# Four-layer gated model on one core: layer 2's mixture by kept picks in blocks of 256, in place of all experts on all tokens

## The chip, the cores and the metric

The kernel runs on one core of a Trainium2 chip, as one program. The metric is the device time of an execution in microseconds. The engines are named as the profile names them: PE is the matrix engine (PEld its weight loads), DVE the vector engine, ACT the scalar engine, POOL the general engine that also issues indirect DMAs, SP the engine that here issues all other DMAs.

## The reference

Four layers follow one another on an activation x of 4 batches x 512 tokens x 256 features, all float32. Each layer adds a gated attention over a context and then a gated feed-forward part, both on a layer norm of x:

```python
x = x + tanh(g_xattn[l]) * attention_l(layernorm(x), ctx)
x = x + tanh(g_ffn[l]) * ffn_l(layernorm(x))
```

Attention 0 is a recurrence over 512 steps (an attention and two LSTM cells in each step); attention 1 is a two-way gated attention; attention 2 is additive (a tanh of the sum of a projected token and a projected context row); attention 3 has 16 heads. The feed-forward part 0 is a mixture with the best expert of 8, part 1 with the best two, part 3 a matrix product on values quantised to 8 bits. The one that is changed is part 2. It keeps, for each token, the experts of highest probability as long as their cumulative probability is under 0.8, and always the best:

```python
probs = softmax(x @ Wr + br)
mask = cumsum(sorted(probs)) < 0.8;  mask[..., 0] = True
gate = probs * keep                                   # keep: mask in the order of the experts
h = relu(einsum('bth,ehf->betf', x, W1) + b1)         # 256 -> 1024, 8 experts
y = einsum('betf,efh->beth', h, W2) + b2              # 1024 -> 256
out = einsum('bte,beth->bth', gate, y)
```

An expert that a token doesn't keep has gate 0 and so adds nothing to it.

## The kernel before, in words

P = 128 is the number of partitions, S = 512 the tokens of a batch, D = 256 the features (KD = 2 pieces of 128), TPB = 4 the pieces of 128 tokens in a batch. The tokens x stay in the chip's memory as `xtok`, 16 pieces of 128 x 256.

**The first part** (`lstm`, `recurrence`) runs the 512 steps of layer 0's attention. What has no place in a step's chain, layer 0's own mixture above all, is put as small tasks into a planner (`Later`) that fills the gaps of the engines. Its weights come through `fetch` and `take`, from SP. This part ends some 3600 us after the start.

**The rest** ("the tail", layers 1 to 3) is written as Python generators, each of which yields after a few instructions. `weave(main, side, ratio)` takes a step of the main generator and then `ratio` steps of the side one, until both have ended; `run` takes one alone; `chain` puts several one after the other. PE's instructions keep the order in which they are written (`InOrder`, L913); the other engines' order is decided by the scheduler of the framework. PSUM is shared by pools of 3 banks for `ps_up`, 2 for `ps_down`, 2 for everything else (`ps_side`) and 1 accumulator. All matmuls of the tail are recorded at L921, so that they are told apart by tile.

- `norm` (L952) makes the layer norm `xn` of a batch and its transpose `xT`.
- `ranked` (L1001) makes the router's values and each expert's rank; `ready_moe` (L1037) adds the keep rule, `comb` (gate times tanh of the layer's factor) and the b2 term.
- `moe` (L1074) is layer 2's mixture for one batch: for each of 8 experts, 8 pieces of 128 hidden features, each two matmuls of 512 columns and a relu on ACT (L1085); then for each of the 4 token pieces, 8 matmuls of 256 columns, whose sum DVE multiplies by the expert's column of `comb` and adds to `xtok` (L1092). All tokens go through all experts. An expert's up and down weights are 1 MB each and are loaded once per batch by SP into two pools of three buffers.
- `Picks`, `picks`, `picked` and `back` (L1113 to L1342) are layer 1's mixture, which works on chosen tokens alone. The tokens are in two groups of 1024. `picks` counts each expert's tokens with two matmuls, makes a place for each (token, expert) pick on DVE, and turns places into a list of tokens by 16 matmuls of one-hot matrices made on DVE (`hot` L1221, `val` L1223). `picked` runs 20 blocks of 128 picks, each gathering its rows by an indirect DMA (`xg`, L1261) from a copy of the normed rows in DRAM, and writes the products to `res` in DRAM (L1311); a branch behind it (L1320) would run up to three more blocks. `back` gathers two rows per token (`yg`, L1331) and adds them to `xtok` with their weights (L1336).
- `additive` (L1544) is layer 2's attention of a batch: 128 ACT tanh (L1565) of 128 x 512, each reduced by PE into `psr`.
- `context_l3`, `heads` (L1693) and `quantised` (L1756) are layer 3: keys and values of the context, then per batch the 16 heads, then the quantised product and the output.

The order of the tail is written out in `gated_blocks_kernel` (L1793): 

1. layer 1's attention and picks of group 0, alone;
2. layer 1's blocks of group 0, woven 1:1 with attention and picks of group 1 and layer 2's context;
3. layer 1's blocks of group 1, woven 1:2 with the gathering back of group 0, `additive` of batch 0, `ready_moe` of batch 0, `additive` of batch 1;
4. `moe` of batches 0, 1, 2 and 3, each woven with what is ready: batch 0 with the gathering back of group 1, `additive` 2 and `ready_moe` 1; batch 1 with `additive` 3 and `ready_moe` 2; batch 2 with `ready_moe` 3, layer 3's context and layer 3 of batches 0 and 1; batch 3 with layer 3 of batch 2;
5. layer 3 of batch 3, alone.

## Time and profile before

| what | value |
|---|---|
| median of three runs | 5609.78 us (5602.8 to 5616.77) |
| the profiled execution | 5608.65 us |
| its span, from the first to the last instruction | 5606.9 us |
| granted PE clock, mean over the span | 0.976 of full speed |
| PE busy | 4908.2 us, 88% of the span |
| DVE, ACT, POOL busy | 2364.6, 2586.2, 284.2 us |
| 0 to 3600 us (recurrence): PE busy | 3077.5 us |
| DMA | 312.55 MB, mean 56 GB/s |
| packets of the indirect DMAs (queue q0) | 3456, 9.44 MB |

A row of the page's groups names a line of the kernel, an engine, an operation, what it writes and reads, how often, its busy time and the mean duration of one. A row of the table by stage gives, for a stretch of the span, the busy time of each engine, the granted PE clock, the share of the DMA engines' time and what they moved. Ends of matmuls are modelled, so that busy times of groups of matmuls overlap a little. Idle time of an engine is put down to the event that ended it.

### The profile page before, as it was taken

The page shows a single profiled execution, that of the slowest core. Times are in us where ns is not written, and L with a number is a line of the kernel's source. Part 1 is how long each engine was busy: PE and PEld are TensorE (multiplying, and loading weights), DVE is VectorE, ACT ScalarE, POOL GpSimd, SP SyncE. Part 2 cuts the span into 40 slices and gives each one's busy share as a digit, 9 for nine tenths or more (in the row PEclk, how much of TensorE's full clock was granted, in tenths as well). Part 3 has the DMA queues.
Part 4 walks back from the last instruction along what each step waited for, and adds up shares of the span by engine and source line. Part 5 has one row for each costly group of instructions (what it writes and reads, how often), then busy time and mean ns, then how long its engine had stood idle before and what let it go on. Part 6 is the DMA issues. An engine that isn't in the chain of part 4 may idle for free. (4 is left out here: it accounts for less than half of the span.)

```text
span 5606.9 us, 137186 instructions
## 1 busy us (share of the span) xinstructions
PE 4908.2 (88%) x57896; PEld 2594.7 (46%) x57896; DVE 2364.6 (42%) x9440; ACT 2586.2 (46%) x7090; POOL 284.2 (5%) x700
## 2 busy tenths in 40 slices
PE   5556798889998899999999899879899999999997
PEld 2222344344444444444444346745344565655664
DVE  4555555555555555555555553144332011232223
ACT  2323464465655665665665565212466545212221
POOL 1000000100000100000000100000101000000000
PEclk9999999999999999999999999979899999999997
DMA  3000010101111111111111112225443112110100
GB/s 114 2 2 2 10 55 32 36 32 39 47 52 39 39 51 40 43 54 40 48 42 40 44 46 97 80 69 177 148 143 115 61 63 92 53 49 31 63 33 5
DMA packets 72766, 312.55 MB, mean 56 GB/s; under 512 B 11361, under 2 KB 27122, under 8 KB 46386
## 3 DMA queue, kind: packets, MB, share of 16 engines
q1 hardware_dynamic: 68690, 294.31, 15.2%
q8 instruction: 454, 7.44, 0.6%
q0 software_dynamic: 3456, 9.44, 0.5%
q14 instruction: 166, 1.36, 0.1%
HBM read 292.18 MB, written 10.22 MB: 54 GB/s over the span
## 5 line engine op out<-in xcount | busy, mean ns | idle before, releaser
L852 PE MATMUL psf<-fw,alb 128*4 128x256 f32 x8192 | 538.4, 380 | 156.4 <-DVE alb L848 125.9
L705 PE MATMUL ps_up<-xm,up 128*128 128x256 f32 x2048 | 614.8, 412 | 3.4 <-ACT h L715 3.3
L736 PE MATMUL ps_down<-down,h 128*128 128x256 f32 x2048 | 580.6, 399 | 0.0
L810 PE MATMUL psf<-whh,hb 128*4 128x256 f32 x8176 | 538.3, 381 | 0.0
L921 PE MATMUL ps_up<-xT,up 128*128 128x512 f32 x1024 | 480.7, 610 | 0.0
L921 PE MATMUL ps_down<-down,h 128*128 128x256 f32 x2048 | 462.0, 382 | 0.0
L705 PEld LDWEIGHTS ps_up<-xm,up 128*128 128x128 f32 x2048 | 335.9, 188 | 226.7 <-issue 174.1
L840 ACT ACTIVATE al<-psr,stat 128x64 f32<-128x64 f32 x1024 | 312.4, 309 | 269.9 <-DVE stat L839 269.3
L736 PEld LDWEIGHTS ps_down<-down,h 128*128 128x128 f32 x2048 | 356.9, 189 | 156.9 <-issue 111.6
L819 ACT ACTIVATE e<-e 128x256 f32<-128x256 f32 x512 | 213.4, 417 | 465.4 <-DVE e L818 464.3
L921 PEld LDWEIGHTS ps_down<-down,h 128*128 128x128 f32 x2048 | 385.0, 190 | 85.4 <-issue 22.2
L801 PE MATMUL psa<-wh,hb 128*4 128x64 f32 x8176 | 208.6, 220 | 228.5 <-DVE hb L878 227.2
L839 DVE TENSOR_REDUCE stat<-psr 128x1 f32<-128x64 f32 x1024 | 229.4, 224 | 417.4 <-PE psr L828 406.6
L818 DVE TENSOR_TENSOR e<-fproj,hw 128x256 f32<-128x256 f32 x1024 | 395.1, 427 | 17.6
L828 PE MATMUL psr<-e,vrep 128*32 128x64 f32 x16384 | 348.7, 223 | 49.0 <-ACT e L819 43.5
L1565 ACT ACTIVATE h<-featT,txtT 128x512 f32<-128x512 f32 x512 | 328.5, 711 | 134.7 <-PE psr L921 125.7
L459 PE MATMUL psf<-ge,ident 128*4 128x256 f32 x4096 | 318.0, 382 | 65.4 <-DVE gt L860 65.2
L828 PEld LDWEIGHTS psr<-e,vrep 128*32 128x32 f32 x16384 | 261.1, 109 | 238.1 <-ACT e L819 230.7
L863 ACT ACTIVATE ga<-gt 128x32 f32<-128x32 f32 x512 | 116.8, 228 | 524.9 <-DVE gt L860 524.7
L860 DVE STREAM_TRANSPOSE gt<-psf 128x256 f32<-128x256 f32 x512 | 230.1, 449 | 301.1 <-PE psf L852 300.5
L852 PEld LDWEIGHTS psf<-fw,alb 128*4 128x4 f32 x8192 | 116.6, 84 | 502.4 <-DVE alb L848 502.1
L1085 ACT ACTIVATE h<-ps_up,m_b 128x512 f32<-128x512 f32 x256 | 175.4, 686 | 375.6 <-PE ps_up L921 375.4
(391 smaller groups left out, 6014.3 us busy)
## 6 DMA issues: line engine op xcount, KB each, us to landing
up<-in_L_w_dram SPq DMA_DIRECT2D x96, 1024.0 KB, 4.9
down<-in_L_w_dram SPq DMA_DIRECT2D x96, 1024.0 KB, 4.9
up<-in_L_w_dram SPq DMA_DIRECT2D x80, 512.0 KB, 4.6
down<-in_L_w_dram SPq DMA_DIRECT2D x40, 512.0 KB, 3.7
res<-y SPq DMA_DIRECT2D x40, 128.0 KB, 6.1
xtok<-in_x_dram SPq DMA_DIRECT2D x4, 512.0 KB, 4.0
xh<-in_x_dram SPq DMA_DIRECT2D x32, 64.0 KB, 2.3
xtok<-xh SPq DMA_DIRECT2D x32, 64.0 KB, 2.0
```

The source lines that it names most:

```text
L459: net.tc.keep_in_program_order(net.nc.tensor.matmul(out[32 * q : 32 * q + NB, :], lhsT=sel, rhs=ge[t // 32][:, ts(q, 256)], start=True, st ...
L705: yield nc.tensor.matmul(cell["ps"][:, f % 2, :], lhsT=ex["w"][:, k, ts(f, P)], rhs=box["x"][:, k, :], start=k == 0, stop=k == KD - 1,)
L736: yield nc.tensor.matmul(cell["ps"], lhsT=ex["h"][:, f, ts(p, P)], rhs=ex["down"][:, f, :], start=f == 0, stop=f == 7,)
L810: pin(nc.tensor.matmul(psf[32 * q : 32 * q + NB, :], lhsT=h[:, c, :], rhs=w["whh"][:, c, ts(q, 256)], start=False, stop=False,))
L818: pin(nc.vector.tensor_add(e[:, p], w["fproj"][:, p], bc(hw[:, :, ts(p, 2)], 3, SC)))
L828: pin(nc.tensor.matmul(ps["r"][p][ts(2 * b + i, 32), :], lhsT=w["vrep"][:, c, :], rhs=ev[:, ::-1, :] if i else ev, start=c == 0, stop=c == ...
L839: pin(nc.vector.tensor_reduce(stat[:, p, 0:1], ps["r"][p], AX.X, ALU.max, negate=True))
L840: pin(nc.scalar.activation(al[:, p], ps["r"][p], AF.Exp, bias=stat[:, p, 0:1], accum_out=stat[:, p, 1:2]))
L852: pin(nc.tensor.matmul(psf[32 * q : 32 * q + NB, :], lhsT=alb[:, p], rhs=w["fw"][:, p, ts(q, 256)], start=False, stop=p == 1,))
L860: pin(nc.vector.transpose(gt.rearrange("p g b -> p (g b)"), psf))
L921: return lambda *a, **k: self.tc.keep_in_program_order(fn(*a, **k))
L1565: nc.scalar.activation(h, featT[:, ec, :], AF.Tanh, bias=w["txtT"][:, ec, col : col + 1])
```

## The change

Layer 2's mixture is computed for kept picks alone, in the manner of layer 1's, and both layers share the code.

- **Groups and kinds.** Layer 2 too works on two groups of 1024 tokens. A `Kind` holds for a layer how many picks a token has at most (2 and 6), the size of a block (128 and 256 picks), how many blocks always run (20 and 20), and how many each nested branch adds (3 and 4), up to 23 and 31 blocks in all.
- **Places.** `picks` makes counts by two matmuls, as before, and a place for each of a token's `most` picks on DVE. The one-hot matmuls and the token list are gone.
- **Putting rows in place.** The normed rows themselves (`xs`) are written to the picks' places in a DRAM array `rows` by indirect DMAs from POOL (L1225 of the new kernel): for each of 8 pieces of 128 tokens, `most` DMAs of 128 rows of 1 KB. That is 16 in a group of layer 1 and 48 in one of layer 2. They are declared independent of each other. A pick that isn't kept goes to a row of its own behind the blocks. A block's rows are then read by one plain DMA on SP (L1277), and each such load waits for all puts of its group.
- **Blocks.** `Blocks` loads rows and weights by the block's expert (a value read by SP), into one ring of three buffers for up and down weights, which replaces the weight pools of the whole kernel. A layer-2 block is 4 transposes, 16 matmuls of 256 columns, 16 relus shared between ACT and DVE, 16 matmuls of 256 columns, and two copies of 128 x 256 (one on DVE, one on ACT) that SP writes to `res`.
- **Branches.** After the sure blocks, `rest` reads the number of blocks and opens nested branches, with one buffer each.
- **Back.** `back` gathers six rows for each piece of 128 tokens in layer 2, 48 per group, through four buffers.
- **Scratch.** All of `rows` and the part of `res` that the sure blocks don't write are filled from x by DRAM-to-DRAM DMAs on SP when the recurrence starts. These are 2 x (14080 + 2817 + 2944 + 385) rows of 1 KB, 41 MB.
- **Order of the tail.** Layer 1's blocks of group 1 are woven 1:2.7 with group 0's gathering back, attention 2 and picks; layer 2's blocks of group 0 1:1.5 with the same of group 1; its blocks of group 1 1:0.75 with the gathering back of group 0, layer 3's context and the first 95 steps of layer 3 of batches 0 and 1. Then `turns` alternates the rest of that, followed by layer 3 of batch 3, with layer 3 of batch 2, which gets the ring's memory and `ps_up`'s banks (`over=True`).

The diff, cut to its core:

```diff
-        self.weights = ctx.enter_context(tc.tile_pool(name="weights", bufs=3))
+        self.ring = keep.tile([P, 3, 2, 2048], FP, name="ring")
+        self.at = {"up": 0, "down": 0}
         self.ready = {part: deque() for part in ("up", "down")}
         self.coming = {part: deque() for part in ("up", "down")}
-        self.expect(0, NBLK)
...
+    def scratch(self, name, rows, unset):
+        x = self.dram.tile([rows, D], FP, name=name)
+        while unset < rows:
+            n = min(NT, rows - unset)
+            self.nc.sync.dma_start(x[unset : unset + n, :], self.a["x"][0:n, :])
+            unset += n
+        return x
...
+KINDS = {1: Kind(1, 2, 128, 20, 3), 2: Kind(2, 6, 256, 20, 4)}
...
+class Kind:
+    def __init__(self, layer, most, size, sure, step):
+        self.layer, self.most, self.size, self.sure, self.step = layer, most, size, sure, step
+        self.all = GB * S * most // size + NE - 1
+        self.none = self.all * size
+        self.rows = self.none + (most * GB * S if most > 2 else 0)
...
     ps = t.ps(P, 2, GJ, NE)
-    mm(nc, ps[:, 0], [(pk.upper, sel)])
-    mm(nc, ps[:, 1], [(pk.ones, sel)])
...
+    place, index = tile("place", kind.most, GJ), tile("index", kind.most, GJ, dt=I32, of="got")
+    cw = tile("cw", kind.most, GJ, of="got")
+    at = tile("at", GJ, NE)
+    for k in range(kind.most):
+        v.scalar_tensor_tensor(at, rank, float(k), pos, ALU.is_equal, ALU.mult)
+        v.tensor_reduce(place[:, k, :], at, AX.X, ALU.add)
+    v.tensor_copy(index, place)
+    to = index
+    if layer == 2:
+        away, to = tile("away", kind.most, GJ), tile("to", kind.most, GJ, dt=I32)
+        v.scalar_tensor_tensor(away, place, kind.none - 0.5, pk.each, ALU.is_gt, ALU.mult)
+        v.tensor_add(away, away, place)
+        v.tensor_copy(to, away)
+    out["put"] = []
+    for j in range(GJ):
+        for k in range(kind.most):
+            x = nc.gpsimd.indirect_dma_start(
+                out=rows[:, :], out_offset=bass.IndirectOffsetOnAxis(ap=to[:, k, j : j + 1], axis=0),
+                in_=xs[:, j, :], in_offset=None,
+            )
+            for y in out["put"]:
+                net.tc.declare_no_dep(x.ins, y.ins, reason="each pick has a place of its own")
+            out["put"].append(x)
+    yield
...
-    ps = t.ps(P, NP1)
-    for k in range(2):
-        for j in range(GJ):
-            hot = two.tile([P, P], FP, name="hot")
-            v.tensor_scalar(hot, pk.col, place[:, k, j : j + 1], None, ALU.is_equal)
-            val = two.tile([P, NP1], FP, name="val")
-            v.tensor_scalar(
-                val, pk.col[:, 0:NP1], blk[:, k, j : j + 1], pk.tok[:, j : j + 1],
-                ALU.is_equal, ALU.mult,
+    v.tensor_copy(tile("expert", kind.all, dt=I32, of="got"), eb)
+    v.tensor_reduce(tile("sum", 1), nb, AX.X, ALU.add)
+    v.tensor_copy(tile("blocks", 1, dt=I32, of="got"), out["sum"])
+    for k in range(kind.most):
+        v.scalar_tensor_tensor(at, rank, float(k), comb, ALU.is_equal, ALU.mult)
+        v.tensor_reduce(cw[:, k, :], at, AX.X, ALU.add)
...
+        b["x"] = self.t.rows[:, at]
+        x = sp.dma_start(
+            b["x"][:, 0 : kind.size // P, :],
+            got["rows"][ts(i, kind.size), :].rearrange("(h p) d -> p h d", p=P),
+        )
+        for y in got["put"]:
+            net.tc.add_manual_dep(
+                x.ins, y.ins.name,
+                mybir.DependencyInfo(mybir.DependencyClass.Sync, mybir.DependencyReason.DATA),
+                reason="the rows' places are known on the chip alone",
             )
...
+    def work_2(self, lo, hi, at):
+        t, nc, w, pool = self.t, self.t.nc, self.w, self.pool
+        nf = F_MOE[2] // P
+        for i in range(lo, hi):
+            b = w[i]
+            h = pool.tile([P, nf, 256], FP, name="h_2")
+            for fp in range(nf // 2):
+                ps = t.up.tile([P, 2, 256], FP, name="ps_up", tag="up")
+                for n in range(2):
+                    f = 2 * fp + n
+                    mm(nc, ps[:, n, :], ((b["up"][:, k, ts(f, P)], b["xT"][:, k, :]) for k in range(KD)))
+                    if n:
+                        nc.vector.tensor_scalar(
+                            h[:, f, :], ps[:, n, :], b["b1"][:, f : f + 1], 0.0, ALU.add, ALU.max
+                        )
+                    else:
+                        nc.scalar.activation(h[:, f, :], ps[:, n, :], AF.Relu, bias=b["b1"][:, f : f + 1])
+                yield
+            self.behind(i, hi, "up", at)
+            if i + 1 < hi:
+                self.turn(w[i + 1])
+                yield
+            for half in range(2):
+                ps = t.down.tile([P, D], FP, name="ps_down", tag="down")
+                mm(nc, ps, ((h[:, f, ts(half, P)], b["down"][:, f, :]) for f in range(nf)))
+                self.out(i, half, ps)
+                if half:
+                    self.behind(i, hi, "down", at)
+                yield
...
+    def rest(self):
+        kind, net = self.kind, self.t.net
+        n = net.nc.values_load(self.got["blocks"][0:1, 0:1], min_val=0, max_val=kind.all)
+        at = (self.first + kind.sure + 2) % 3
+        def go(lo):
+            if lo < kind.all:
+                with net.tc.If(n > lo):
+                    hi = min(lo + kind.step, kind.all)
+                    run(self.some(lo, hi, at))
+                    go(hi)
+        go(kind.sure)
...
+    for b in batches:
+        for i in range(TPB):
+            j = (b - group[0]) * TPB + i
+            for k in range(kind.most):
+                y = pool.tile([P, D], FP, name="yg", bufs=4)
+                nc.gpsimd.indirect_dma_start(
+                    out=y[:, :], out_offset=None, in_=got["res"][:, :],
+                    in_offset=bass.IndirectOffsetOnAxis(ap=got["index"][:, k, j : j + 1], axis=0),
+                )
+                xj = net.xtok[:, b * TPB + i, :]
+                nc.vector.scalar_tensor_tensor(
+                    xj, y, got["cw"][:, k, j : j + 1], xj, ALU.mult, ALU.add
+                )
+            yield
...
-            run(layer1(0))
-            weave(picked(t, pk, pairs[0]), chain(layer1(1), context_l2(t, w2, p2)), 1.0)
...
+            run(picks_of(1, 0, l1))
+            weave(b0.sure(), chain(picks_of(1, 1, l1), context_l2(t, w2, p2)), 1.1)
+            b0.rest()
...
-        weave(
-            picked(t, pk, pairs[1]),
-            chain(back(t, pk, 0, pairs[0]), additive(t, w2, p2, 0), second(0), additive(t, w2, p2, 1)), 2.0,
-        )
-        net.expect(2, NB)
-        for _ in range(3):
-            net.fetch()
-        weave(moe(t, m2, 0, got[0]), chain(back(t, pk, 1, pairs[1]), additive(t, w2, p2, 2), second(1)), 1.0)
-        weave(moe(t, m2, 1, got[1]), chain(additive(t, w2, p2, 3), second(2)), 1.0)
...
+        weave(b1.sure(), chain(back_of(1, 0), picks_of(2, 0, l2)), 2.7)
+        b1.rest()
+        weave(c0.sure(), chain(back_of(1, 1), picks_of(2, 1, l2)), 1.5)
+        c0.rest()
...
-        return chain(heads(t, w3, p3, b), quantised(t, w3, p3, b, out))
-    weave(
-        moe(t, m2, 2, got[2]),
-        chain(second(3), context_l3(t, w3, p3), layer3(0), layer3(1)), 1.35,
-    )
-    weave(moe(t, m2, 3, got[3]), layer3(2), 0.6)
-    run(layer3(3))
+    def layer3(b, over=False):
+        return chain(heads(t, w3, p3, b, over), quantised(t, w3, p3, b, out))
+    start = chain(back_of(2, 0), context_l3(t, w3, p3), layer3(0), layer3(1))
+    weave(c1.sure(), part_of(start, 95), 0.75)
+    c1.rest()
+    run(turns(
+        chain(start, back_of(2, 1, [3]), layer3(3)),
+        chain(back_of(2, 1, [2]), layer3(2, True)),
+    ))
```

## The prediction

> **What bounds the kernel now.** I read the slices of the page first, then its groups, then a table by stage, then the chain of waits and the POOL timeline in single stages. In the slices, each 140 us long, TensorE is only half to nine tenths busy in the first 26 (the recurrence, which the diff leaves alone but for its start) and full in the ones that hold layer 2.
>
> ```profile
> PE   5556798889998899999999899879899999999997
> PEclk9999999999999999999999999979899999999997
> ```
>
> The table by stage (columns: stretch, its length, then busy us and count of PE, PEld, DVE, ACT, POOL, granted clock, DMA share, GB/s) covers everything after the recurrence and the first layer-1 attentions:
>
> ```profile
> 3741.00:3966.00 225.00, 206.42 (x756) 121.44 (x756) 98.79 (x262) 46.14 (x77) 17.85 (x19) 0.96 0.44 147
> 3966.00:4010.00 44.00, 21.66 (x40) 9.68 (x40) 16.19 (x39) 5.23 (x7) 21.00 (x22) 0.61 0.58 200
> 4247.00:4274.00 27.00, 16.90 (x37) 7.62 (x37) 15.51 (x48) 7.55 (x15) 11.91 (x13) 0.81 0.67 260
> 4274.00:5491.00 1217.00, 1187.43 (x4725) 728.36 (x4724) 247.61 (x572) 413.48 (x643) 1.09 (x1) 0.99 0.16 56
> 5491.00:5607.00 116.00, 77.21 (x321) 52.02 (x320) 42.61 (x81) 21.16 (x33) 0.00 (x0) 0.69 0.01 5
> ```
>
> The 1217 us of layer 2's mixture are PE time: 1187 busy at a clock of 0.99. So a matmul removed there comes off the end one for one. The stretches that lose time are the seams: the first weave's end (44 us with 22 busy, clock 0.61), the second's (27 with 17), and layer 3's last batch alone (116 with 77, clock 0.69). The chain (start, us, what) gives the price of a piece with nothing modelled in it; I use it and not the busy sums of the groups, whose modelled ends overlap (480.7 + 462.0 = 942.7 us):
>
> ```profile
> 5434.99 10.50 PE ps_up L921 x24
> 5445.49 3.45 PE ps_down L921 x16
> ```
>
> **Removed: 32 (expert, batch) pieces.** 24 records of ps_up are 12 matmuls of 512 columns in 10.50 us, so four take 3.50; 16 records of ps_down are 8 matmuls of 256 columns in 3.45. A piece has 16 of the first and 32 of the second: 4 x 3.50 + 4 x 3.45 = 27.8 us, x32 = 890.
>
> **Added: 40 blocks of 256.** A block has 16 up matmuls and 16 down matmuls, all of 256 columns: 32 x 3.45/8 = 13.8 us, and four transposes of rows (x8 records took about 1.05 us at full clock): 14.85, x40 = 594. The reference's inputs give 4333 kept picks in the first 1024 tokens, by expert 35, 996, 965, 641, 66, 991, 155, 484: 1+4+4+3+1+4+1+2 = 20 blocks; the second group also fills 20. The nested branches are never entered, and a token keeps at most 5, so the sixth pick is always spare work. **Saved: 890 - 594 = 296 us.**
>
> Here a rule speaks against the change. The Trainium skill, "TensorE: Matmul & The Clock Gate", section "Why this matters for your kernels", asks that narrow matmuls (M under 512) be padded or looped densely over K, or the clock oscillates. The change halves the width of ps_up. At half clock all the time the 594 would be 1188, and the kernel about 300 us slower than before. The row for it is ps_down: 256 wide, 3.45 us for 16 records in the middle of a stretch whose clock is 0.99. I take the row; width alone costs nothing while PE has a queue.
>
> **Added: indirect DMAs on POOL, and the seams.** Today's 72 (40 xg, 32 yg) become 128 scatters (2 x 16 and 2 x 48) and 128 gathers. The POOL timeline (start, us, engine, line, operation, idle before it) at the second seam:
>
> ```profile
> 4245.29 0.96 POOL L1331 DMA_INDIRECT yg<-res,g_index  x1 [0.30 <-issue]
> 4246.55 0.95 POOL L1331 DMA_INDIRECT yg<-res,g_index  x1 [0.30 <-issue]
> ```
>
> One each 1.26 us where nothing is waited for; 16 gathers with four buffers and their additions took 25.4 us, 1.6 each. No scatter is in the trace. The nearest row is this gather: 1.26 from issue to issue, and a median of 4.3 from issue to landing (2.7 to 6.1). From below a scatter can't be cheaper than POOL's 0.95. From above, each is paid to its landing. The skill, "DMA: Bandwidth & Descriptors", "Anatomy of one DMA - SWDGE (gpsimd) path", has 2.0 us fixed plus bytes/436e3, 2.3 us for 128 KB, mostly the receipt of the write and most for HBM, the target here. One after another, 48 would take 110 us by it, 60.5 by the row. The scatters are declared independent, so I take the row, and the rule for the upper side. Seam by seam, with PE kept in program order and the place of each instruction read off the changed kernel's order:
>
> - First: token lists took 3727 to 3738 (16 one-hot pairs), the gather 3.2 more. Now 16 scatters, 20 us, about 4 to land and 2.5 for the row load: +12.5. The second group's lists disappear from the first weave, where they held PE some 12 us: net 0.
> - First weave to second: the branch and the wait for weights stay as in the 44 us stretch. 0.
> - Layer-1 blocks to layer-2 blocks: the scatters follow their counts by about 11 us on DVE; 60.5 + 4 + 2.5 to the first row load: first transposes at +79. PE has two layer-1 blocks left (about 22 us): 56 idle, which replaces the 10 idle of 4247 to 4274. +46.
> - First to second half of layer 2: same queue, with 40 us of blocks left. 45 idle, less what the old kernel lost here, nothing. Layer 3's 4 MB of weights stand ahead of block 1's on SP: at about 400 GB/s some 8 us more. A memset of context_l3 stands on DVE behind all scatters and ahead of the last relu, so the last down matmuls (7 us) fall behind the wait; that is inside the 45. +53.
> - End: layer 3 of batch 2 needs 24 gathers of 1.6 us, the last landing (4) and a norm (6), while about 8 us of batch 1 are left: 40 idle, and 28 later, where batch 3 runs out its own chain. The old end idled 39. +29.
> - Clock: after the idle of 3966 to 3973, eight records took 6.68 us instead of 3.50. Three new idles: 3 x 4 = +12.
> - The second half's additive attentions now stand beside 20 blocks where they stood beside 16 pieces of twice the PE work. A batch has 128 tanh of 0.71 us, two batches 182 us of ACT, plus relus and copies, under 380 of PE. I charge +15 for places where the weave meets ACT, and +6 for the gathers that the second group's norm waits for, behind POOL's scatters.
>
> Sum: -296 + 0 + 46 + 53 + 29 + 12 + 21 = -135.
>
> At no cost: the fills. 41 MB from DRAM to DRAM go out on SP at the recurrence's start; the DMA view shows 2 GB/s from 70 to 560 us and SP's next issue at 665, so they need some 65 GB/s; the first slice moved 227 GB/s at a share of 0.63. At half that pace they end some 600 us late, the first mixture's weights queue behind them on SP, and the work that fills the recurrence's gaps runs after it instead: up to 600 us. Sixteen relus of half the old width (0.69 us for 512) are some 6 us on two engines under 13.8 of PE, two copies of y replace two additions into xtok (0.49); uncovered they would cost about 1 us a block, 40 in all. DVE's loops for places (12 operations of about 0.25) are counted in the 11 us. Block traffic is 2.25 MB per 14.85 us, 151 GB/s, against 400 seen.
>
> **How the numbers follow.** The profiled execution took 5608.65 us with a span of 5606.9, so 1.7 lie outside the span; the median, 5609.8, is 1.1 above it. 5606.9 - 135 + 1.7 + 1.1 = 5475.
>
> - Forecast, seams as priced: 5475. Chance 0.60, own range 5430 to 5520.
> - The seams hide better: if the picks finish early enough in each weave that POOL's 60 us run under blocks, 46 + 45 and most of the clock's 12 go: about 5380. The order speaks against it (the picks end two blocks before the weave does), the unknown pace of PE in the weave for it. 0.12.
> - Scatters at the rule's 2.3 us: 1.04 more for each of the 96 of layer 2, which are exposed, is +100, and 17 more if the first seam's 16 are too: 5575 to 5590. Speaks for it: HBM writes with receipts; against: the four independent gathers at 1.26. 0.15.
> - Slower than before: POOL waits for each scatter before the next (the ring, or a dependency that the declaration does not lift). At the landing of 4.3 us, (4.3 - 1.26) x 112 exposed = +340: about 5815. The turn is at 135/112 = 1.2 us above the row, 2.5 us per scatter. Against it: the gathers' 0.30 gaps and two landings in flight. 0.08, with the fills delaying the recurrence inside it.
> - It doesn't do what it says: 21 blocks in a group would run a branch with one buffer, each block waiting for 2 MB (about 25 us in series), up to 100 us a group, 5575 to 5675. The count excludes it unless rounding moves picks over a boundary (the first group's expert 5 has 991 of 1024, expert 6 155 of 256: far off). 0.02. A time within 0.3% of before, which is about what a measurement of this kernel can tell from no change: 0.03 of all.
>
> The range leaves out the lower half of the well-hidden case, the slow case and what lies beyond: 5390 to 5590. Faster by over 0.3%: 0.88; within: 0.03; slower: 0.09.
>
> **What the profile after would show.** PE's groups: layer 2's up and down matmuls of 256 columns, 1280 records each of ps_up and ps_down in the 40 blocks, about 3.45 us for 16 at a clock of 0.99; two idle PE stretches of 45 to 60 us, ended by a row load; POOL with 48 DMA_INDIRECT in a row at 1.26; an idle of about 40 us before batch 2's norm. I am wrong if the gaps on POOL exceed 0.3 us, if blocks stand more than 16 us apart with PE idle inside (weights or x rows late), or if the recurrence ends later than it does now.

## The result, and the profile after

The changed kernel takes 5827.24 us, the median of four runs (5819.72 to 5830.31), against 5607.39 for the kernel before on the same chip: a ratio of 1.0388 [1.037, 1.0406]. It is slower. The profiled execution took 5819.72 with a span of 5818.0, at a mean clock of 0.941. The forecast span was 5606.9 - 135 = 5471.9, so the miss is 346 us.

The slices of the changed kernel, 145 us each:

```profile
PE   3455689889999899999999899868884888398857
PEclk7899999999999999999999999889996999699967
```

Where layer 2 stood at 9s before, slices 31 and 35 (the seams) are at 4 and 3 tenths, the three slices between at 8, and the clock is 6 in both seams and in slice 39, near the end. The table by stage, for the row of scatters ahead of layer 2's first group, its blocks, the seam between the groups, the second group's blocks, and the end (columns as before):

```profile
4407.00:4475.00 68.00, 0.00 (x0) 0.00 (x0) 5.24 (x13) 0.00 (x0) 49.36 (x52) 0.53 0.54 187
4475.00:4938.00 463.00, 400.96 (x1928) 259.68 (x1928) 112.13 (x310) 219.95 (x382) 20.56 (x22) 0.97 0.32 108
4938.00:5032.00 94.00, 17.26 (x66) 13.10 (x66) 8.45 (x21) 2.54 (x6) 39.48 (x41) 0.60 0.45 168
5032.00:5524.00 492.00, 424.05 (x1860) 313.99 (x1860) 138.36 (x290) 80.66 (x155) 40.71 (x41) 0.97 0.32 104
5524.00:5818.00 294.00, 191.42 (x840) 126.15 (x840) 131.89 (x278) 54.38 (x85) 47.16 (x48) 0.72 0.11 28
```

The two seams hold 145 us without PE (68 and 94 - 17), where the forecast had 109. In the two block stages PE is idle for 62 and 68 us although the clock is 0.97.

The first seam is the row of 48 scatters and what follows it: POOL's last scatter, SP's loads of the blocks' rows, and PE's first transposes.

```profile
4458.34 0.96 POOL L1225 DMA_INDIRECT rows<-g_xs,g_to  x1 [0.31 <-issue]
4472.07 3.49 SPq L1277 DMA_DIRECT2D rows_in<-rows  x3
4475.09 1.09 PE L932 MATMUL ps_side<-ident,rows_in 128*128 128x128 f32 x4 [68.10 <-DMA rows_in<-rows]
```

The load went out 12.8 us after the last scatter was issued (4458.34 + 0.96), where 4 had been forecast. The PE timeline about the second seam (start, us, what, idle before it and what ended it) shows two more kinds of loss:

```profile
4911.65 7.07 PE L932 MATMUL ps_down<-ring,h 128*128 128x256 f32 x32
4918.56 1.03 PE L932 MATMUL ps_up<-xT,ring 128*128 128x256 f32 x4
4920.20 1.99 PE L932 MATMUL ps_up<-xT,ring 128*128 128x256 f32 x8 [0.61 <-ACT h L1390]
4922.76 1.99 PE L932 MATMUL ps_up<-xT,ring 128*128 128x256 f32 x8 [0.56 <-ACT h L1390]
4925.32 1.99 PE L932 MATMUL ps_up<-xT,ring 128*128 128x256 f32 x8 [0.56 <-issue]
4927.88 1.13 PE L932 MATMUL ps_up<-xT,ring 128*128 128x256 f32 x4 [0.56 <-issue]
4928.85 0.60 PE L932 MATMUL ps_side<-ident,rows_in 128*128 128x128 f32 x4
4929.28 7.07 PE L932 MATMUL ps_down<-ring,h 128*128 128x256 f32 x32
...
4937.68 0.47 PE L932 MATMUL ps_up<-xT,ring 128*128 128x256 f32 x1 [0.67 <-issue]
4986.89 3.78 PE L932 MATMUL ps_up<-xT,ring 128*128 128x256 f32 x8 [48.74 <-ACT h L1390]
...
5016.60 1.09 PE L932 MATMUL ps_side<-ident,rows_in 128*128 128x128 f32 x4 [12.22 <-DMA rows_in<-rows]
...
5031.77 2.05 PE L932 MATMUL ps_up<-xT,ring 128*128 128x256 f32 x4 [14.09 <-DVE xT L1316]
```

First kind: a block alone on PE goes from 4911.65 to 4929.28, 17.6 us where 14.85 was forecast. The down matmuls cost what was said (32 records in 7.07). The up matmuls come as x4, x8, x8, x8, x4, with about 0.6 idle before each new group. A piece of 128 features is four records, so every wait lies between the two pieces of a pair, which share one tile of PSUM: the second piece is ordered behind the relu that reads the first. That is on ACT, and took 0.47. A pair takes 2.56 us where its eight records need 1.73 by the forecast's row. In the waits of the whole tail, PE waits for these relus 160.1 us in 156 places, the seam's one long wait included. Second kind: those 48.74 us at once, in the seam; that wait is not for the relu's work but for ACT to start it, as shown below.

A further loss lies at the start of the kernel. SP's timeline at the start (start, us, what, count), and then DVE's waits from 50 to 260 us (what, for what: total, times, longest):

```profile
38.56 17.30 SPq L89 DMA_DIRECT2D rows<-in_x_dram  x7
...
69.44 38.11 SPq L89 DMA_DIRECT2D rows<-in_x_dram  x7
...
122.99 18.45 SPq L509 DMA_DIRECT2D xh<-in_x_dram  x4
...
164.94 0.33 SPq L1605 DMA_DIRECT2D l_vec<-in_L_vec_dram  x1
```

```profile
DVE wslide L1621 <- DMA l_vec<-in_L_vec_dram: 96.4, 1, 96.4
```

SP issues the 41 MB of fills until 116 us, then loads for layer 0's mixture that stand behind them, and only at 164.94 asks for `l_vec`, a small constant of layer 2's attention. DVE's copy of it is written in `context_l2`, which belongs to the tail; the scheduler had moved it into the fifth step of the recurrence (the text on record for k1 says the third). In the kernel before, load and copy both came behind the recurrence, at 3441.3 and 3444.2 us; what let the scheduler take them so early here isn't shown. DVE takes its instructions in their order, so the chain of 512 steps stood behind this copy for 96.4 us. The last step's first product on PE comes at 3537, before at 3434.

### The profile page after: what moved, and what is told of

Its sections match the earlier page's. It is cut to its first block, busy times and chain, and to the rows that moved or that the text cites. A ratio compares the mean times of both kernels' runs of the same rounds, so it can differ in the third digit from the quotient of the medians.

```text
span 5818.0 us, 138301 instructions
## 1 busy us (share of the span) xinstructions
PE 4685.9 (81%) x57488; PEld 2527.6 (43%) x57488; DVE 2463.7 (42%) x9688; ACT 2511.3 (43%) x7042; POOL 465.4 (8%) x884
## 5 line engine op out<-in xcount | busy, mean ns | idle before, releaser
L716 PE MATMUL ps_up<-xm,ring 128*128 128x256 f32 x2048 | 614.8, 412 | 3.4 <-ACT h L726 3.3
L747 PE MATMUL ps_down<-ring,h 128*128 128x256 f32 x2048 | 583.2, 401 | 0.0
L932 PE MATMUL ps_up<-xT,ring 128*128 128x256 f32 x1280 | 361.7, 413 | 178.0 <-ACT h L1390 160.1
L716 PEld LDWEIGHTS ps_up<-xm,ring 128*128 128x128 f32 x2048 | 335.9, 188 | 226.7 <-issue 174.1
L747 PEld LDWEIGHTS ps_down<-ring,h 128*128 128x128 f32 x2048 | 358.4, 190 | 157.2 <-issue 111.9
L829 DVE TENSOR_TENSOR e<-fproj,hw 128x256 f32<-128x256 f32 x1024 | 395.4, 427 | 17.6
L932 PEld LDWEIGHTS ps_up<-xT,ring 128*128 128x128 f32 x1280 | 234.0, 198 | 315.9 <-ACT h L1390 225.6
L890 POOL COPY cb<-ga 128x8 f32<-128x8 f32 x512 | 97.0, 189 | 3314.9 <-DVE ga L882 3314.9
L812 PEld LDWEIGHTS psa<-wh,hb 128*4 128x4 f32 x8176 | 114.0, 86 | 486.7 <-DVE hb L889 486.7
```

Of the source, the lines that this page charges most:

```text
L716: yield nc.tensor.matmul(cell["ps"][:, f % 2, :], lhsT=ex["w"][:, k, ts(f, P)], rhs=box["x"][:, k, :], start=k == 0, stop=k == KD - 1,)
L747: yield nc.tensor.matmul(cell["ps"], lhsT=ex["h"][:, f, ts(p, P)], rhs=ex["down"][:, f, :], start=f == 0, stop=f == 7,)
L812: pin(nc.tensor.matmul(ps["a"][32 * q : 32 * q + NB, :], lhsT=h[:, c, :], rhs=w["wh"][:, c, ts(q, 64)], start=c == 0, stop=c == 1,))
L829: pin(nc.vector.tensor_add(e[:, p], w["fproj"][:, p], bc(hw[:, :, ts(p, 2)], 3, SC)))
L932: return lambda *a, **k: self.tc.keep_in_program_order(fn(*a, **k))
```

## The experiments

The experiments ran on several chips. The kernel before took 5605 to 5609 us on each, so a few us between runs of different chips are not read as an effect. The theory after the result, A in the texts on record, has three places: (1) the constants' copies behind the fills, (2) the shared bank, (3) rows of scatters during which the other engines see each other's signals late. Its rivals have the other letters; each text says what they hold of its run. The chief ones are that any long row of indirect DMAs does what scatters do, and that a memset, not the signals, sets the end of the seam.

**k1_pinned and k2_banks: one place each, in the changed kernel.** In k1 the constants' instructions keep their written place:

```diff
-    nc.vector.memset(w["wslide"], 0.0)
-    nc.vector.tensor_copy(w["wslide"][:, :, 31], w["vec"][:, 0, :])
+    pin = net.tc.keep_in_program_order
+    pin(nc.vector.memset(w["wslide"], 0.0))
+    pin(nc.vector.tensor_copy(w["wslide"][:, :, 31], w["vec"][:, 0, :]))
```

and likewise the copies to `rep` and `off`. In k2 each piece has a bank of its own:

```diff
-                ps = t.up.tile([P, 2, 256], FP, name="ps_up", tag="up")
                 for n in range(2):
...
-                    mm(nc, ps[:, n, :], ...)
+                    ps = t.up.tile([P, 1, 256], FP, name="ps_up", tag="up")
+                    mm(nc, ps[:, 0, :], ...)
```

> The changed kernel with one thing altered: the copies that put layer 2's constants in place (wslide, rep, off) are pinned behind what DVE was given before them. Theory A: in the changed kernel the copy of l_vec into wslide stood on DVE among the third step of the recurrence and waited 96 us for a small load that SP had queued behind the 41 MB of fills; the whole recurrence moved by the 103 us that its last step shows. Then this kernel takes 5827 - 103 = 5724 us, and its recurrence ends near 3437 us. Rival B: the fills slow the recurrence by their traffic or hold up loads that it needs, so that pinning a copy gives less than 20 us.

> The changed kernel with one thing altered: each piece of 128 hidden features of a layer-2 block gets a PSUM bank of its own, where two pieces shared one. Theory A: in a shared bank the second piece's matmuls wait for the relu that reads the first; four such waits of about 0.7 us make a block 17.6 us where its matmuls need 14.9, 2.8 x 40 = 112 us. Some is hidden where other work is woven in: PE's waits for that relu sum to about 100 us. Then this kernel takes 5827 - 100 = 5727 us (5710 to 5740) and blocks with nothing beside them stand 15 us apart. Rival B: the relus on ACT and DVE, or the weights, set the pace of a block; then under 20 us go.

Measured: k1 5724.6 us (5719.76 to 5733.53), 103 less than the changed kernel, ratio to before 1.0215 [1.0198, 1.0232]. The fills are still there and still take SP's time; only the copy moved, as the tile view of `l_vec` shows (issue by SP, and the copy):

```profile
L1605 SPq DMA_DIRECT2D l_vec<-in_L_vec_dram x1: 328/328/328, 170.5 to 170.5; - x1
L1622 DVE COPY wslide<-l_vec x1: 169/169/169, 3932.5 to 3932.5; 128x2 f32<-128x2 f32 x1
```

So place 1 is shown. The last step's first product comes at 3438, and the 4 us that are left against before are the most that the fills by themselves can cost there. k2 took 5691.65 us (5689.71 to 5699.59), 136 less, ratio 1.0157 [1.0141, 1.0174]. Its PE timeline over a block with nothing beside it, from one down product to the next:

```profile
4840.00 7.07 PE L932 MATMUL ps_down<-ring,h 128*128 128x256 f32 x32
4846.90 7.07 PE L932 MATMUL ps_up<-xT,ring 128*128 128x256 f32 x32
4853.81 0.60 PE L932 MATMUL ps_side<-ident,rows_in 128*128 128x128 f32 x4
4854.25 7.07 PE L932 MATMUL ps_down<-ring,h 128*128 128x256 f32 x32
```

No idle stands between the pieces any more: the 32 up records take 7.07 in one run, 3.54 for 16, within 3% of the forecast's row. The block alone takes 14.25 us, where the changed kernel's took 17.63. Place 2 is shown. It was worth more than the 100 expected, which had been read from the sum of PE's waits; 40 blocks at the difference of 3.38 make 135, an estimate from these two lone blocks that agrees with the 136 measured.

**b_scatter and b_gather: the row alone, in the kernel before.** In the fourth expert of batch 1's old mixture, 48 indirect DMAs that nobody waits for are put on POOL; everything else is as before:

```diff
+            for k in range(48):
+                x = nc.gpsimd.indirect_dma_start(
+                    out=far[:, :], out_offset=bass.IndirectOffsetOnAxis(ap=to[:, k : k + 1], axis=0),
+                    in_=src[:, :], in_offset=None,
+                )
```

b_gather has 48 gathers of rows of x into eight tiles in their place.

> The kernel before, with 48 independent scatters of 128 rows added on POOL in the middle of layer 2's mixture of batch 1, where PE always has queued work; their source is a tile of zeros and their target an array that nobody reads. Theory A: while POOL scatters, signals between the other engines arrive late (in the changed kernel PE's signals of 4932.9 and 4936.4 us were seen at 4958.0 and 4986.1), so PE stops although nothing depends on the scatters: 48 x 1.27 = 61 us, less what is still queued, +40 to +65 us over before (5650 to 5670). Rival B: the stall in the changed kernel comes from a dependency of its own; then scatters beside queued work cost nothing, 5607 +- 8 us.

> The kernel before, with 48 gathers of 128 rows from the input into eight tiles that nobody reads, at the same place as the scatters of the companion run. Theory A: only scatters hold up the other engines' signals; 48 gathers cost 0 to 8 us. Rival C: any long row of indirect DMAs on POOL does it; then +40 to +65 us as for scatters.

Measured: 5651.57, ratio 1.008 [1.0063, 1.0097], +46 us; and 5654.03, ratio 1.0087 [1.007, 1.0104], +49 us. Both rows do it, and the part of the theory that named scatters alone fell. The PE timeline with the relu on ACT that it waited for, and the table by stage, of b_scatter, whose row runs from 4620.0 to 4679.9:

```profile
4644.33 1.98 PE L921 MATMUL ps_up<-xT,up 128*128 128x512 f32 x4
4671.27 0.69 ACT L1087 ACTIVATE h<-ps_up,m_b 128x512 f32<-128x512 f32 x1 [16.08 <-remote]
4672.01 3.78 PE L921 MATMUL ps_up<-xT,up 128*128 128x512 f32 x4 [25.69 <-issue]
```

```profile
4620.00:4640.00 20.00, 17.95 (x79) 10.31 (x78) 1.45 (x3) 5.68 (x9) 15.43 (x16) 1.00 0.41 151
4640.00:4660.00 20.00, 6.31 (x16) 1.48 (x15) 0.00 (x0) 3.19 (x5) 15.12 (x17) 0.69 0.26 104
```

For the first 16 DMAs PE is busy for 17.95 of 20 us. From about 4646 us on, some 20 DMAs into the row, PE, DVE and ACT nearly stop together, with DMA at 0.26 of its time. ("Remote" means that the profile has a signal just then, but no instruction that ended near it. The relu reads a product that PE had finished by 4646.3.)

**b_paced, b_twelve, b_thin: how many, and how fast.** The same 48 scatters with a small POOL operation behind each (on 128 x 256 in b_paced, on 128 x 1 in b_thin), and the first 12 of them alone:

```diff
+                pin(nc.gpsimd.tensor_scalar(idle, src, 1.0, 0.0, ALU.mult, ALU.add))
```

> As b_scatter (the kernel before with 48 idle scatters beside layer 2's mixture of batch 1), but behind each scatter POOL works on a tile of 128 x 256 for about 1.2 us, so that scatters start some 2.5 us apart instead of 1.27. In b_scatter PE worked on for the first 13 to 16 scatters and then stood still. Theory D: scatters started faster than they are finished pile up, and what piles up holds the other engines' signals; at half the pace nothing piles up: 5605 to 5615 us, although the scatters now take 120 us. Rival E: each scatter holds the others up for a time of its own, so the 46 us that b_scatter lost are lost here too: 5645 to 5660 us.

> As b_scatter, but 12 scatters in place of 48, at the same pace of 1.27 us. Theory D: the row is over before anything has piled up: 5605 to 5612 us. Rival E, a price for each scatter: 46 x 12/48 = 12 us, 5617 us.

> As b_paced (48 idle scatters beside the mixture of the kernel before, POOL working on a tile behind each), but that work is on 128 x 1 in place of 128 x 256. In b_paced the work took 0.42 us, so scatters started 1.62 us apart (not 2.5), and nothing was lost; in b_scatter they started 1.27 apart and 46 us were lost. Theory D, the pace decides: the starts are now some 1.4 us apart, between the two, and 15 to 46 us are lost (5625 to 5655). Rival F: what decides is that POOL does something else between two scatters, at whatever pace: 5600 to 5615 us.

Measured: 5608.65, 1.0 [0.9991, 1.0008]; 5608.22, 0.9999 [0.999, 1.0008]; 5606.76, 0.9998 [0.999, 1.0007]. All three cost nothing. b_paced's pitch was 1.62 us, not the 2.5 that its text supposed (the operation took 0.42). The POOL timeline of b_thin, then its table by stage:

```profile
4640.94 1.01 POOL L1854 DMA_INDIRECT far<-x_src,x_to  x1 [0.17 <-issue]
4641.98 0.20 POOL L1863 TENSOR_SCALAR x_idle<-x_src 128x1 f32<-128x1 f32 x1
4642.35 1.01 POOL L1854 DMA_INDIRECT far<-x_src,x_to  x1 [0.17 <-issue]
```

```profile
4640.00:4660.00 20.00, 20.00 (x73) 7.88 (x73) 0.00 (x0) 16.99 (x28) 17.20 (x29) 1.00 0.43 158
```

At a pitch of 1.42 us, PE is busy for the whole of the stretch in which b_scatter has 6.31. So the row costs nothing at this pace in this kernel, and theory D's 15 to 46 us did not come. Whether it is the slower pace or the other operation between two DMAs was not told apart, since every slower row had such an operation.

**k3_both, k4_five: both mends, then five picks.** k3 is k1 and k2 together. k4 also gives layer 2 five picks per token, the most that any token keeps here, so 40 scatters and 40 gathers in a group:

```diff
-KINDS = {1: Kind(1, 2, 128, 20, 3), 2: Kind(2, 6, 256, 20, 4)}
+KINDS = {1: Kind(1, 2, 128, 20, 3), 2: Kind(2, 5, 256, 20, 4)}
```

> The changed kernel with both alterations, pinned constants and a PSUM bank for each piece. They lie in different stages, so their gains of 103 and 136 us should add: 5827 - 103 - 136 = 5588 us, 0.3% under before. If one hides the other, 5620 us or more.

> As k3_both, with five picks for a token in place of six; a token keeps at most five. 40 scatters and 40 gathers in a group instead of 48 each. Theory: at both layer-2 seams PE waits for the whole row of scatters, so 8 x 1.27 x 2 = 20 us go there, and 4 gathers of 1.6 us ahead of layer 3's batch 2 give 6 more: 5562 us. If the seams are held by something else (the branch, the weights), under 8 us go: 5580 us or more.

Measured: k3 5547.65 (5544.85 to 5550.2), ratio 0.9887 [0.987, 0.9903]: the change now gains. That is 41 us better than the sum of the two parts. By the traces of k2 and k3, 98 of the 140 us between them lie in the recurrence, 19 from there to the first group's first product, 16 from the second row of scatters to the last up product and 8 behind it; why the last three are there is open. k4 took 5515.71 (5513.99 to 5518.25), ratio **0.983 [0.9814, 0.9847]**, the best of the study, faster than both kernels.

**What ends the seam: a_memset, a_thin.** In the changed kernel the memset of layer 3's `ones` stands on DVE in the seam and needs memory that the scatters still read. a_memset pins it later; a_thin also puts the 128 x 1 operation behind every scatter.

```diff
-    nc.vector.memset(w["ones"], 1.0)
+    net.tc.keep_in_program_order(nc.vector.memset(w["ones"], 1.0))
```

> The changed kernel with one thing altered: the memset of layer 3's row of ones, whose memory is free only when all of the second group's scatters have landed, is pinned behind the gathers' additions instead of standing on DVE ahead of the last blocks' relus. Theory A: in the changed kernel PE's late signals hold the seam to the end of the scatters in any case, so nothing goes: 5827 +- 8 us. Theory G, the memset is what holds the last block: 20 to 35 us go, 5792 to 5807 us.

> As a_memset, with a POOL operation on 128 x 1 behind every scatter of both layers, which in the kernel before took the whole price of 48 scatters away (b_thin). Theory A: with signals in time and the memset out of the way, the last blocks run beside the row of scatters: about 17 us at the seam between the halves of layer 2 and 13 us in the first weave (PE idle 4049 to 4062 us) go, while rows of 48 take 7 us longer: 5795 to 5812 us. If the signals play no part in the changed kernel, it equals a_memset or is some us slower.

Measured: 5777.35 (5762.89 to 5781.53), 1.0304 [1.0287, 1.0321], 50 less than the changed kernel; and 5794.95, 1.0335 [1.0318, 1.0353], 32 less, but 18 more than a_memset. The profile of a_memset, which is of its fastest run, puts only some 16 us of the gain in the seam; 21 lie ahead of the first group's first product and 9 in that group's blocks, where I can't assign them to the edit. Nor did the edit free DVE. In the waits of DVE, the cast to `identb`, which needs the same memory, has taken the memset's place, in a_memset and then in a_thin:

```profile
DVE identb L1773 <- DMA rows<-g_xs,g_to: 36.6, 1, 36.6
DVE identb L1778 <- DMA rows<-g_xs,g_to: 42.9, 1, 42.9
```

PE waited 32.3 and 38.6 us for a relu behind that cast. So neither kernel tests the pace.

**Tries to get the seams out of k4.** Four kernels change the weave or the row: k5_ratio takes 2.2 steps of the second group's picks per block step in place of 1.5; to k5, k6_paced adds a 128 x 256 POOL operation behind that group's scatters; to k6, k7_tail keeps 30 steps of layer 3 for the end; k8_all has k4 with ratio 1.9, the pinned memset and 128 x 1 operations behind all scatters.

```diff
-        weave(c0.sure(), chain(back_of(1, 1), picks_of(2, 1, l2)), 1.5)
+        weave(c0.sure(), chain(back_of(1, 1), picks_of(2, 1, l2)), 2.2)
```

```diff
+        if layer == 2 and batches[0]:
+            pin(x)
+            pin(nc.gpsimd.tensor_scalar(pk.idle, xs[:, j, :], 1.0, 0.0, ALU.mult, ALU.add))
```

```diff
-        weave(c1.sure(), part_of(start, 95), 0.75)
+        weave(c1.sure(), part_of(start, 95 - AHEAD), 0.75 * (95 - AHEAD) / 95)
+        run(back2); run(part_of(last, 2)); run(part_of(start, AHEAD))
```

> As k4_five (5516 us), with the second group's attention and picks woven at 2.2 side steps to a step of the first group's blocks in place of 1.5, so that the picks end some 8 blocks (120 us of PE) ahead of the half's end and the 40 scatters run beside blocks. In k4_five PE stood 68 us at this seam (28.8 + 14.6 + 15.2 + 9.2). Theory A: a row of scatters at 1.27 us stops PE whatever is queued, from the 13th or so on: (40 - 13) x 1.27 = 34 us stay, and the 24 us behind the branch stay too, so 5500 to 5512 us. Rival: nothing but the dependency holds PE there; then 43 us go, 5465 to 5478 us.

> As k5_ratio, with POOL working on a 128 x 256 tile behind each scatter of the second group of layer 2, which puts the starts 1.62 us apart. Theory A: the other engines are no longer held up, and the row of 40 (65 us) lies beside blocks: about 34 us under k5_ratio and 40 to 50 under k4_five, 5462 to 5478 us. Rival: the pace makes no difference here, since the row's own dependency holds PE; then it equals k5_ratio within 8 us or is slower.

> As k6_paced, with 30 steps of layer 3 of batch 1 kept out of the weave with the last blocks and put behind the gathers for batch 2, where PE stood 13.4 + 11.9 us in k4_five and had half its clock. If these idles are only a matter of order: 20 to 30 us under k6_paced. If the gathers' additions on DVE stand ahead of layer 3's softmax and hold it, nothing or a loss of up to 20 us.

> The four repairs together (pinned constants, a bank for each piece, five picks, pinned memset), with a POOL operation of 128 x 1 behind each scatter and the second group's picks woven at 1.9. In k6_paced PE's signals came in time, but PE stood 33 us from 4695 to 4728 us, until the memset was through. If the memset held it, most of these 33 us go: 5482 to 5500 us. If something else is next, it stays at 5516 to 5525 us like k4_five to k6_paced.

Measured: 5520.93 (.9837 [.982, .9853]), 5525.32 (.9849 [.9833, .9866]), 5559.97 (.9909 [.9893, .9926]), 5526.99 (.9859 [.9842, .9875]). None beats k4, and k7 loses 35 to k6. PE's timeline and DVE's wait in k6, then the same in k8, say why the slower row gained nothing:

```profile
4727.91 2.50 PE L932 MATMUL ps_down<-ring,h 128*128 128x256 f32 x5 [33.13 <-DVE h L1392]
DVE ones L1761 <- DMA rows<-g_xs,g_to: 38.1, 1, 38.1
```

```profile
4750.11 2.50 PE L932 MATMUL ps_up<-xT,ring 128*128 128x256 f32 x5 [28.18 <-DVE h L1391]
DVE identb L1779 <- DMA rows<-g_xs,g_to: 36.8, 1, 36.8
```

With the slower row no signal in the seam is late, and PE waits all the same, for a relu on DVE. In k6 DVE stood at the memset of `ones` until the scatters had landed; in k8 that memset was out of the way and the cast to `identb` stood in its place, as in a_memset.

**k9_clear, k10_fast: the pace, with DVE clear.** k9 is k8 with that cast pinned, and the DVE step behind it (the absolute value of layer 3's weights); k10 is k9 without the POOL operations.

```diff
-    nc.vector.tensor_copy(w["identb"], net.ident)
+    net.tc.keep_in_program_order(nc.vector.tensor_copy(w["identb"], net.ident))
```

> As k8_all, with layer 3's other early steps on DVE (the cast of the identity, the absolute value of the weights) pinned behind what DVE was given before them, too. In k8_all the memset was out of the way, and the cast of the identity, whose memory also comes free with the last scatter, had taken its place: PE stood 28 us until it was through. With nothing on DVE waiting for the scatters, the row lies beside blocks: 20 to 28 us under k8_all, 5499 to 5507 us. If still another step takes its place, 5520 to 5530 us.

> As k9_clear, without the POOL operation behind each scatter, so that scatters start 1.27 us apart again. Theory A, scatters at this pace hold the signals up and stop PE from the 13th or so on: 27 x 1.27 = 34 us more than k9_clear at this seam, less the 6 us that each shorter row saves: 20 to 35 us over k9_clear. Rival: with the waits of DVE gone the pace makes no difference: within 8 us of k9_clear.

Measured: k9 5527.7 (5515.56 to 5543.88), .985 [.9833, .9866]; k10 5550.99 (5545.32 to 5566.46), .9902 [.9883, .9921]. So the slower row is worth 23 us in the change's own setting (the two spreads just fail to meet). The waits of PE in k9 and in k10 about that seam, the longest of each:

```profile
PE ps_up L932 <- DVE h L1391: 7.5, 2, 7.3
```

```profile
PE ps_up L932 <- ACT h L1390: 37.9, 1, 37.9
```

In k9's row PE stands for 10.0 and 4.6 us in place of k10's 37.9, so the stall is shorter but not gone. The longer one, on PE, and the copy on ACT ahead of the relu that it waits for:

```profile
4753.45 8.32 PE L932 MATMUL ps_up<-xT,ring 128*128 128x256 f32 x20 [9.96 <-issue]
4750.70 0.37 ACT L1327 COPY y<-ps_down 128x256 f32<-128x256 f32 x1 [17.45 <-remote]
```

Signals are late here at a pitch of 1.42 us, at which b_thin lost nothing. From one group's first product to the other's k9 is 21 us faster than k4 (445 against 467). Yet its profiled span, of the slowest of its four executions, is 25 above k4's (its median 12): the other stages take 15 us more up to the first product, 21 in the second group's blocks and 10 in the end. What they pay for is open.

## Why the prediction was wrong

The forecast gives no times by stage. By an estimate that lays its sums on the trace before, the 346 us are 103 in the recurrence, 16 up to the first group's first product, 91 from there to the second group's, 75 in the second group's blocks, 48 in the end (333; the rest is in the first weaves). By its steps:

- **"At no cost: the fills" is the step that failed most surely.** Its DMA argument held: SP had issued the 41 MB by 116 us, the DMA engines were busy to about 170, and with the copy moved (k1) the recurrence's last step comes 4 us later than before, far from the 600 of the upper bound. But I looked only for work that would queue behind the fills on SP by need. What mattered was a constant that nobody needs for 3500 us, whose load stood behind the fills and whose copy stood inside the recurrence. The place to look was DVE's order within the recurrence: does any instruction there read a DMA that is queued after the fills? Price: 103 us, by k1.
- **"A block is 14.85 us" failed: 17.6 alone.** The matmul rate was right (7.07 for 32 records in k2, where the block takes 14.25), and so was taking the row over the rule about narrow matmuls: the granted clock is 0.97 in both block stages, so the loss isn't the clock's. The sum had only PE's work in it. I costed the relus as hidden "under 13.8 of PE" by comparing amounts, not by asking who is ordered behind each; the old ps_up was one piece of 512 to a bank, the new one two of 256, the second behind the first's relu. Price: 136 us, by k2, of the 296 that were to be saved. My sign for being wrong ("blocks more than 16 us apart with PE idle inside") pointed at this, but blamed weights and rows.
- **The seams were undersized:** idle 56 and 53 forecast, 68 and 77 measured, and the first weave, forecast at nothing, has a 13.0 us idle of PE of its own. The scatters cost what I took from the gather's row (1.27 us a scatter, 61 us for 48, gaps of 0.30). POOL didn't wait for one to land before the next, at the 2.3 us that I estimated from the Trainium skill ("DMA: Bandwidth & Descriptors", "Anatomy of one DMA - SWDGE (gpsimd) path") or at the 4.3 of the slower rival. As a time to land, that estimate agrees with the 2.4 (median) that the profiles of b_twelve, b_paced and b_thin give; for the fast rows of 48 the profile gives no landing. The slower rival's 5815 lies 3 us from the span, and its mechanism isn't in the trace at all: a right number for a wrong reason. What failed at the first seam is a size: 12.8 us from the last scatter to the row load, for 4; why they are 12.8 is open. What failed at the second is the assumption that the blocks left over run under POOL's row. By their modelled ends, PE's last two down products were done at 4932.9 and 4936.4; DVE and ACT, idle, took them at 4958.0 and 4986.1. The timelines of DVE, then of ACT, in the changed kernel:

```profile
4958.06 0.42 DVE L1324 COPY y<-ps_down 128x256 f32<-128x256 f32 x1 [23.92 <-remote]
```

```profile
4986.09 0.37 ACT L1322 COPY y<-ps_down 128x256 f32<-128x256 f32 x1 [58.26 <-remote]
```

  ACT's next instruction behind this copy, a relu, was what PE waited for. A full buffer of `y` is not the cause: of the semaphores (the counters by which engines signal) that the two copies wait for, the trace has the last updates of all others by 4934.2, and PE's at 4958.0 and 4986.1. b_scatter and b_gather show that such a row costs 46 to 49 us by itself; k10 less k9 gives 23 in the change.
- **The memset that waits for the scatters** was in the forecast ("inside the 45"). It, or the cast behind it, holds DVE until the row has landed, and PE with it: 33 and 28 us in k6 and k8 with no late signal, 28.8 in k4 with the fast row. So it covers the same stretch as the late signals, and what removes one leaves the other. Only k9, with both eased, has the shorter stall.
- **The end: +29 forecast, 294 us against about 246 meant.** It holds 191 us of PE work at a clock of 0.72. k7 tried to fill it and lost 35. Its cause was not tested further.
- **No branch was entered and the blocks were 40**, as said.

With the two mends, which leave the change's idea alone, it is k3: 5547.65, still 73 above the forecast of 5475; the seams and the end are what is left to explain that rest, but no experiment splits it. Not settled: how a row of indirect DMAs delays the signals, k3's 41 us beyond the sum of its parts, and the small differences outside the seam in a_memset and k9.

## What to carry to other kernels

When a change puts large transfers on a queue early, list every later issue on that queue and where the first reader of each stands on its own, in-order engine: a constant copy hoisted into a serial chain costs the whole delay, however late its result is used. When a tile is halved, look at what now shares a PSUM bank or buffer, and price a block by its handoffs and not by the sum of one engine's work. A time that hits a rival's number proves nothing of its mechanism until an experiment has moved that mechanism alone.

## What the runs showed of the hardware that had not been expected

- 48 indirect DMAs in a row at 1.27 us each, scatters or gathers, cost work that has no part in them 46 to 49 us. The delay sets in some 12 DMAs into the row in the changed kernel and some 20 in b_scatter. In the same kernel 12 cost nothing, and 48 at 1.42 us with a 0.20 us POOL operation between them cost nothing either. In k9 a row of 40 at 1.42 us with such operations still left PE standing for 10.0 and 4.6 us, so this pace is no sure remedy. It isn't DMA bandwidth: the DMA engines were busy 0.26 of the time while the stall of b_scatter lasted, and 0.43 in the same stretch of b_thin, without one.
- During such a row, DVE and ACT took PE's products 25 and 50 us after their modelled ends (the changed kernel). Whether the signals were given late or arrived late, the trace does not tell.
- A scatter of 128 rows of 1 KB landed 2.4 us (median) after its issue in b_twelve, b_paced and b_thin, while b_twelve's were issued every 1.27 us.
